# Attention tail of a hyperbolic transformer block: o is scaled ahead of its transpose, TensorE adds the output bias, and the gate product and |a|^2 read the projection from PSUM

## The chip, the cores and the metric

The kernel runs on one core of one Trainium2 chip. A core has five engines that work side by side, each through its own queue in order: TensorE (PE in the profile, with its weight loads as PEld), VectorE (DVE), ScalarE (ACT), GpSimd (POOL) and SyncE (SP, which here issues the DMAs). The metric is the device time of one execution in microseconds, taken as the median of three runs.

## The reference, cut to what matters

Two layers are computed for x of 128 sequences by 64 tokens by 256 features (8192 tokens). Layer 0 is a recurrent scan over the 64 tokens and a quantised feed-forward. Layer 1 is an attention block in hyperbolic space, followed by a small feed-forward and a quantised linear layer. The change lies in the end of the attention:

```
out_h    = expmap0(softmax(q k / 4) v)             # 16 heads of 16 features
attn_out = plin(_from_heads(out_h), w_o, b_o)      # plin: expmap0(logmap0(x) @ w + b)
attn_t   = g_msa * logmap0(attn_out)
x        = mobius_add(residual, expmap0(attn_t))
```

With o the 256 features that leave the softmax for one token, and full a factor for that token that follows from |o|^2, the projection is a = full * (o @ w_o) + b_o. For expmap0 and logmap0 the kernel needs, for every token, |a|^2, the product g_msa * a, and |g_msa * a|^2. They are row sums, one number for each token.

## The kernel before, in words

The tokens are cut into 64 tiles of 128 tokens, and the tiles into 16 groups of 4 (GT = 4), each group into 2 pairs of tiles. A first stage runs the scan, a second the feed-forward of layer 0, and the last, `fused`, does the rest and is the longest.

`fused` is a software pipeline over the groups. Its loop counter k runs from -5 to 18, and in each pass it writes, in this order: `tail(k)` (the residual sums and the scale factors behind attention of group k and behind the small feed-forward of group k - 3), `norms(k)` (layer norm and modulation), `fp6` (the last linear layer of group k - 3), `mlp(k)`, `attention(k + 5)` and `front(k + 6)` (the way in from layer 0). So attention is written five groups ahead of the `tail` that reads it. Written order is not the order of execution: the compiler's scheduler sorts all instructions of an engine by an estimate of their times, with the small coefficient chains (`radial`, `ln_coeffs`, `tail_coeffs`) given priority, and each engine then runs its list strictly in that order. Semaphores hold an instruction until what it reads is written and what it overwrites is free.

PSUM has eight banks, and the table CFG gives them out by name: qk 2, sc 2, ao 1, dn 1, ml 1, fp 1. The one bank called ao serves all of the second half of attention. A group passes through it in this order: for each of its two pairs, the products of the softmax numerators with v, twice (L983, copied out by ACT at L986); then, for each pair, four transposes of o (L92, copied out by ACT at L1005 as oT) and eight projection products with w_o (L1010), which VectorE reads at L1014. Only then can the next group's L983 write the bank.

Between the last L986 of a group and L1014 lies `full`: VectorE divides by the softmax denominator (L988, L989), ScalarE and VectorE sum the squares of o (`square_sum`, L609 and L611), and `radial` on POOL turns the sums into the factor (L653, L640, L655, tiles fullq and fullr).

Behind L1014, `tail_sums` does three things to each tile: a square sum of a on ScalarE (L609), the product with the gate g_msa on POOL (L737, in place), and a square sum of the result on ScalarE. The gate rows `ada` come by DMA (`load_ada`, kind 2 of block 0, two buffers `ada02`). `mlp` calls the same `tail_sums` for its own gate, also on POOL. Later `x_dot` on VectorE (L743) reads the product.

`rows3` is a bf16 tile in whose rows, in groups of three, biases lie as sums of three bf16 parts; a matmul with a matrix of ones from `ones3` as weights adds such a bias in PSUM (L912, L1036, L1092). The output bias b_o is not among them; it lies in `bo`, copied to all partitions, and L1014 adds it.

Of the kernel before, what the change touches and what calls it, by code (L numbers as in the profile page):

```python
# [11 lines left out]
F32 = mybir.dt.float32  # L12
F32R = mybir.dt.float32r
BF16 = mybir.dt.bfloat16
# [3 lines left out]
ALU = mybir.AluOpType  # L18
# [4 lines left out]
P = 128  # L23
B, T, D = 128, 64, 256
# [18 lines left out]
NG = NT // GN  # L43
AR = 8
TS = 4
CFG = {'rnd': 'S', 'ef': 8, 'fill': {'x1a': 'V', 'mod0': 'V'}, 'hold': [3, 0], 'mk': 2, 'raw': 1, 'mv': 6, 'xs': 3, 'la': 3, 'sb': 7, 'qks': 'GGGG', 'deq': 'VV', 'first': 1000, 'hb': 2, 'q_h': 'P', 'q_x1': 'P', 'q_xr': 'P', 'q_ot': 'P', 'q_out': 'P', 'q_ada': 'P', 'room': [[0.3, 0.3, 0.55], [0.5, 0.4, 0.2]], 'qv': 64, 'p1': 'GVGVGVGV', 'x1': 3, 'u1': 16, 'u2': 6, 'qkv': 2, 'sq': 1, 'uT1': 2, 'uT2': 2, 'qM': 2, 'kT': 2, 'e': 4, 'oT': 1, 'yT': 1, 'hq': 2, 'hl': 2, 'xr': 1, 'ot': 2, 'ada00': 2, 'ada02': 2, 'ada10': 2, 'ada12': 4, 'dn': 1, 'qk': 2, 'sc': 2, 'ao': 1, 'ml': 1, 'fp': 1, 'mod0': 'GGGV', 'mod1': 'VVVV', 'sqm0': 'SSSS', 'sqm1': 'SSSS', 'su0': 'VVVV', 'su1': 'VGVG', 'q8': 'GGGGGG', 'hqc': 'SSSVVV', 'qm': 'SSSS', 'x1a': 'GV', 'gate0': 'GGGG', 'gate1': 'GGGG', 'yb': 'GG', 'va': 'GGGG', 'sqt': 'SSSS', 'sqg': 'SSSS', 'sqo': 'SSVS', 'f2e': 'SSSS', 'early': 0, 'q8f': 'VVVVVV', 'hqf': 'SSSVVV', 'fl': 1, 'un': 2, 'jsu': 1, 'LA': 5, 'LM': 3, 'tl': 6, 'ord': 1, 'xt': 3, 'q_xt': 'P'}
GT = 4
NGR = NTILE // GT

LA, LM = CFG["LA"], CFG["LM"]  # L50

# [19 lines left out]
def tile_kernel(ctx, tc, a, out):  # L71
    nc = tc.nc
    V, S, G_, PE = nc.vector, nc.scalar, nc.gpsimd, nc.tensor
    dma = nc.sync.dma_start
# [4 lines left out]
    const = ctx.enter_context(tc.tile_pool(name="const", bufs=1))  # L79
# [14 lines left out]
    ones = const.tile([P, P], F32, name="ones")  # L94
    V.memset(ones, 1.0)

    ones3 = const.tile([P, 3, P], BF16, name="ones3")
    V.memset(ones3, 0.0)
    for n in range(3):
        V.memset(ones3[32 * n : 32 * n + 3, n, :], 1.0)  # L100

    mhead = const.tile([P, 4], F32, name="mhead")
# [2 lines left out]
    wt = ctx.enter_context(tc.tile_pool(name="wt", bufs=1))  # L105
# [4 lines left out]
    wo = wt.tile([P, 2, D], F32, name="wo")  # L110
    wfT = wt.tile([P, 2, D], F32, name="wfT")
    wdT = wt.tile([P, 6, D], BF16, name="wdT")
    bo = wt.tile([P, D], F32, name="bo")
    bf2 = wt.tile([P, D], F32, name="bf2")
    bb2 = wt.tile([P, 1], F32, name="bb2")

    rows3 = wt.tile([P, 2 * D], BF16, name="rows3")
    V.memset(rows3, 0.0)
    sdh = wt.tile([P, D], F32, name="sdh")
    cu = wt.tile([P, 1], F32, name="cu")  # L120
# [21 lines left out]
    with ExitStack() as l0:  # L142
# [15 lines left out]
        with ExitStack() as sc_:  # L158
# [3 lines left out]
            setup = sc_.enter_context(tc.tile_pool(name="setup", bufs=1))  # L162
# [84 lines left out]
            def pieces():  # L247
# [7 lines left out]
                for w, sc, dst in ((a["w_gate"], s_g, wgT), (a["w_up"], s_u, wuT)):  # L255
# [8 lines left out]
                    for j in range(6):  # L264
# [3 lines left out]
                        k = P if j < 5 else 64  # L268
# [7 lines left out]
                for j in range(6):  # L276
                    pt = bank()
                    k = P if j < 5 else 64
# [15 lines left out]
                yield 0, 0.3, 0.5  # L294


                dma(out=bo, in_=a["b_o"].partition_broadcast(P))
                dma(out=bf2, in_=a["b_f2"].partition_broadcast(P))
                dma(out=wo, in_=a["w_o"].rearrange("(c p) k -> p c k", p=P))
                r4 = setup.tile([4, D], F32, name="r4")  # L300
# [94 lines left out]
            for i in range(4):  # L395
                va = ep.tile([P, H, 2, HV], F32, name=f"va{i}", tag=f"va{i}", bufs=1)
# [85 lines left out]
        for b0 in range(0, B, NBB):  # L482
            for c in range(2):

                q8 = xp.tile([P, NBB, T], I8, name="q8", tag="q8")
                src = hsT[:, c, :, b0 : b0 + NBB].rearrange("p t b -> p b t")
# [4 lines left out]
                q8f = q8.rearrange("p b t -> p (b t)")  # L491
# [28 lines left out]
        for tb in range(NG):  # L520
            sl = slice(tb * GN, (tb + 1) * GN)
            for j in range(5):
                pg = ps_a.tile([P, GN], F32, name="pgate", tag="pgate")
                pu = ps_a.tile([P, GN], F32, name="pup", tag="pup")
                for ps, w in ((pg, wgT), (pu, wuT)):
                    for c in range(2):
                        PE.matmul(ps, lhsT=w[:, c, j * P : (j + 1) * P], rhs=xqT[:, c, sl],  # L527
                                  start=(c == 0), stop=(c == 1))
                h_chunk(pg, pu, j, tb, h_d[tb, j])
            if tb % 2:  # L530
# [20 lines left out]
def fused(ctx, tc, a, out_tok, x_tok, L):  # L551
    nc = tc.nc
    V, S, G_, PE = nc.vector, nc.scalar, nc.gpsimd, nc.tensor
# [4 lines left out]
    bo, bf2, bb2, rows3, sdh, cu = (L[k] for k in ("bo", "bf2", "bb2", "rows3", "sdh", "cu"))  # L558
# [46 lines left out]
    def square_sum(e, tag, src, acc):  # L605

        junk = pl.tile([P, D], BF16, name="junk", tag=f"junk{tag}{e}", bufs=1)
        if e == "S":
            S.activation(junk, src, AF.Square, accum_out=acc)  # L609
        else:  # L610
            V.scalar_tensor_tensor(junk, src, 1.0, src, ALU.mult, ALU.mult, accum_out=acc)  # L611

    def scale(e, dst, src, by):

        if e == "S":
            S.activation(dst, src, AF.Copy, scale=by)  # L616
# [113 lines left out]
        for g in range(GT):  # L730
            scale(pick(f"su{which}", g), u[g], u[g], su[:, g : g + 1])

    def tail_sums(av, gb, sums, g, which, tag):

        aa2, ga2, _ = sums
        square_sum(pick("sqt", g), f"t{tag}", av, aa2[:, g : g + 1])
        ENG[pick(f"gate{which}", g)].tensor_tensor(av, av, gb, ALU.mult)  # L737
        square_sum(pick("sqg", g), f"t{tag}", av, ga2[:, g : g + 1])

    def x_dot(xs, av, sums, g, tag):  # L740
# [147 lines left out]
    def attention(i, u, sums):  # L888

        i0 = at[0] = i * GT  # L890
        oall = u
# [106 lines left out]
        for h2 in pairs:  # L998
            pt = bank("ao")
            for i in range(2):  # L1000
                for c in range(2):
                    o = (2 * i + c) * P
                    turn(pt[:, o : o + P], oall[2 * h2 + i][:, c * P : (c + 1) * P])
            oT = big("oT", [P, 4, P])
            S.copy(oT.rearrange("p c t -> p (c t)"), pt)  # L1005
            pm = bank("ao")
            for i in range(2):
                g = 2 * h2 + i
                for c in range(2):
                    PE.matmul(pm[:, i * D : (i + 1) * D], lhsT=oT[:, 2 * i + c, :], rhs=wo[:, c, :],  # L1010
                              start=(c == 0), stop=(c == 1))
            for i in range(2):
                g = 2 * h2 + i
                V.scalar_tensor_tensor(av[g], pm[:, i * D : (i + 1) * D], full[:, g : g + 1], bo,  # L1014
                                       ALU.mult, ALU.add)
                gb = load_ada(0, 2, 1, i0 + g)
                tail_sums(av[g], gb[:, 0, :], sums, g, 0, "a")
        return av

    def mlp(i, u, x2, sums):  # L1020

        i0 = at[0] = i * GT
        fn2 = mk("fn2", GT)
        for h2 in pairs:
            uT = big("uT2", [P, 2, 2, 2 * P], F32R)
            pt = bank("ml")
            for c in range(2):
                for i in range(2):
                    o = (2 * c + i) * P
                    turn(pt[:, o : o + P], u[2 * h2 + i][:, c * P : (c + 1) * P])  # L1030
            S.copy(uT[:, 0], two(pt))
            V.tensor_tensor(uT[:, 1], two(pt), uT[:, 0].bitcast(F32), ALU.subtract)
            for i in range(2):
                g = 2 * h2 + i
                pm = bank("ml")
                PE.matmul(pm, lhsT=ones3[:, 2, :], rhs=rows3, start=True, stop=False)  # L1036
                for k in range(2):
                    cs = slice(k * P, 2 * D)
                    for q, (w, z) in enumerate(PASSES):
                        PE.matmul(pm[:, cs], lhsT=uT[:, z, k, i * P : (i + 1) * P], rhs=wm[:, w, k, cs],  # L1040
                                  start=False, stop=(k == 1 and q == 2))
                junk3 = pl.tile([P, D], BF16, name="junk3", tag="junkz", bufs=1)
                V.tensor_tensor_reduce(out=junk3, in0=pm[:, :D], in1=u[g], scale=1.0, scalar=0.0,
                                       op0=ALU.mult, op1=ALU.add, accum_out=fn2[:, g : g + 1])
                if pick("f2e", g) == "S":
                    S.copy(u[g], pm[:, D:])
                else:
                    V.tensor_copy(u[g], pm[:, D:])
        cf = radial(fn2, "cf", plus=bb2)
        av = u  # L1050
        for g in range(GT):
# [3 lines left out]
            tail_sums(av[g], gb[:, 0, :], sums, g, 1, "m")  # L1055
            x_dot(x2[g], av[g], sums, g, "m")
        return av

# [169 lines left out]
```

## Time and profile before

| what | value |
|---|---|
| median of 3 runs | 1380.88 us (1379.86 to 1386.22) |
| the profiled execution's own time | 1374.36 us |
| its span (first to last instruction) | 1372.6 us |
| busy in the span: DVE, PE, POOL, ACT | 1145.4, 1096.8, 844.6, 827.0 us |
| granted TensorE clock, mean | 0.871 |
| gate products L737 on POOL (attention and mlp) | 128 of 827 ns in the mean |
| projection read L1014 on DVE | 64 of 473 ns in the mean |
| square sums L609 on ACT | 432 of 428 ns, each with a read of the accumulator of 203 ns |

A busy share says how much of the span an engine worked; a wait is the idle time in front of one instruction, put down to the instruction that ended it. In a group's line the columns are: line, engine, operation, names written and read, shapes and count, then busy time, mean ns of one, and idle time before it with what ended it.

### The profile page before, as it was taken

What the parts mean: (1) busy time and instruction counts of PE and PEld (TensorE: products, weight loads), DVE (VectorE), ACT (ScalarE), POOL (GpSimd) and SP (SyncE); (2) the same over time, 40 slices, a digit from 0 to 9 for tenths busy, and PEclk for the clock granted to TensorE, in tenths of its full rate; (3) what the DMA queues carried; (4) which work ended last, traced back from release to release, by engine and by line L of the source; (5) the groups of instructions that cost most, each with busy time, mean ns of one, the idle gap of its engine ahead of it and who ended that gap; (6) DMA issues with size and microseconds to landing.
All of it is one profiled execution on the core that took longest, in us unless ns stands there. A gap on an engine that the chain in (4) does not pass through costs nothing.

```text
span 1372.6 us, 23851 instructions
## 1 busy us (share of the span) xinstructions
PE 1096.8 (80%) x7380; PEld 744.0 (54%) x7380; DVE 1145.4 (83%) x3544; ACT 827.0 (60%) x2428; POOL 844.6 (62%) x1043
## 2 busy tenths in 40 slices
PE   7999957984589789878879798888887888964654
PEld 4656542332366566655657576666655656643442
DVE  5666669997778787888998999999899989899573
ACT  2545438982377568666768666776675777752331
POOL 3111207865688766687868878686686785765441
PEclk9999989995599789889999798997998989986765
DMA  7112245669733441233344334322414231323211
GB/s 236 54 54 85 70 196 195 257 265 283 225 96 120 124 145 49 90 116 117 98 130 125 116 113 146 108 92 90 126 63 124 70 104 51 97 74 96 72 47 46
DMA packets 119306, 163.66 MB, mean 119 GB/s; under 512 B 10885, under 2 KB 72074, under 8 KB 119178
## 3 DMA queue, kind: packets, MB, share of 16 engines
q1 hardware_dynamic: 119178, 162.13, 37.0%
q8 instruction: 58, 0.95, 0.3%
q14 instruction: 70, 0.57, 0.1%
HBM read 115.94 MB, written 46.14 MB: 118 GB/s over the span
## 4 chain that ended last, share of the span: by engine, by line
DVE 44%; PE 21%; POOL 14%; DMA 8%; issue 6%; ACT 6%; SPq 1%; POOLq 0%; DVEq 0%; ACTq 0%
DMA ada<-ada_d 5%; PE pg L434 4%; DVE u L797 4%; PE pg L415 3%; DVE u L724 2%; DVE u L725 2%; DVE junk L743 2%; DVE nh L920 2%; DVE u L618 2%; DVE bn L703 2%; DVE u L1052 2%; POOL r L640 2%; PE pgate L527 1%; PE qk L915 1%; POOL u L737 1%
## 5 line engine op out<-in xcount | busy, mean ns | idle before, releaser
L609 ACT ACTIVATE junk<-u 128x256 bf16<-128x256 f32 x432 | 183.8, 428 | 162.1 <-DVE u L725 49.4
L915 PE MATMUL qk<-wqkv,uT 128*128 128x512 f32 (+1 forms) x768 | 194.8, 391 | 12.3 <-DVE uT L906 6.4
L737 POOL TENSOR_TENSOR u<-u,ada 128x256 f32<-128x256 f32 x128 | 105.7, 827 | 80.9 <-ACT junk L609 73.4
L915 PEld LDWEIGHTS qk<-wqkv,uT 128*128 128x128 f32 x768 | 132.9, 209 | 40.2 <-DVE uT L906 12.1
L966 PE MATMUL sc<-qM,kT 64*64 64x256 f32 x1024 | 128.1, 419 | 20.9 <-ACT kT L956 11.6
L1040 PE MATMUL ml<-wm,uT 128*128 128x512 f32 (+1 forms) x384 | 120.9, 454 | 0.0
L983 PE MATMUL ao<-va,e 128*64 128x34 f32 x2048 | 90.1, 241 | 32.9 <-DVE u L1014 17.8
L983 PEld LDWEIGHTS ao<-va,e 128*64 128x64 f32 x2048 | 79.5, 155 | 59.6 <-DVE u L1014 19.4
L1040 PEld LDWEIGHTS ml<-wm,uT 128*128 128x128 f32 x384 | 83.7, 221 | 47.3 <-issue 25.3
L616 ACT ACTIVATE qM<-sc,mhead 128x256 f32<-128x256 f32 x256 | 102.0, 495 | 11.5 <-PE sc L92 11.3
L880 PE MATMUL dn<-wdT,hq 128*128 128x256 bf16 (+1 forms) x384 | 66.3, 314 | 45.9 <-DVE x L882 20.4
L513 POOL TENSOR_TENSOR hv<-uv,sil 128x512 f32<-128x512 f32 x44 | 57.6, 1312 | 66.2 <-DVE am L516 48.5
L945 POOL TENSOR_TENSOR va<-qkv,comb 64x256 f32<-64x256 f32 x128 | 88.3, 690 | 9.9 <-PE ao L983 4.2
L966 PEld LDWEIGHTS sc<-qM,kT 64*64 64x64 f32 x1024 | 56.5, 143 | 63.1 <-ACT kT L956 17.7
L609 ACT ACTIVATION_READ_ACCUMULATOR junk<-u 128x1 f32 x432 | 87.9, 203 | 0.0
L974 ACT ACTIVATE e<-sc 128x512 f32<-128x512 f32 x128 | 74.7, 606 | 19.4 <-PE ao L983 9.7
L434 PE MATMUL pg<-hsT,WT 128*128 128x128 f32 x504 | 75.3, 289 | 9.4 <-ACT hsT L446 9.0
L434 PEld LDWEIGHTS pg<-hsT,WT 128*128 128x128 f32 x504 | 64.7, 191 | 31.4 <-ACT hsT L446 28.6
L1094 PE MATMUL fp<-wfT,yT 128*128 128x256 f32 x256 | 78.7, 439 | 0.0
L941 POOL TENSOR_TENSOR qkv<-qkv,comb 128x512 f32<-128x512 f32 x64 | 70.2, 1110 | 12.3 <-DVE comb L932 3.0
L620 POOL TENSOR_SCALAR hb<-hl,cu 128x1280 int8<-128x1280 f32 x64 | 64.2, 1008 | 21.4 <-DMA hl<-h_d 14.0
L880 PEld LDWEIGHTS <-hq 128*128 128x128 bf16 (+1 forms) x384 | 37.2, 108 | 73.1 <-issue 37.5
(286 smaller groups left out, 3192.6 us busy)
## 6 DMA issues: line engine op xcount, KB each, us to landing
ada<-ada_d SPq DMA_DIRECT2D x128, 256.0 KB, 3.5
h_d<-hv SPq DMA_DIRECT2D x80, 256.0 KB, 2.1
hl<-h_d SPq DMA_DIRECT2D x32, 640.0 KB, 4.3
ada<-ada_d SPq DMA_DIRECT2D x128, 128.0 KB, 2.4
xt<-in_xT_dram SPq DMA_DIRECT2D x16, 512.0 KB, 4.5
xr<-in_x_dram SPq DMA_DIRECT2D x32, 256.0 KB, 4.3
x_d<-x SPq DMA_DIRECT2D x32, 256.0 KB, 3.1
xt<-x_d SPq DMA_DIRECT2D x32, 256.0 KB, 2.8
```

The costliest lines, as they stand in the source:

```text
L434: lp = PE.matmul(pg[c][:, st], lhsT=WT[:, k, c * P : (c + 1) * P], rhs=hp[:, k, :], start=False, stop=False, skip_group_check=True)
L609: S.activation(junk, src, AF.Square, accum_out=acc)
L616: S.activation(dst, src, AF.Copy, scale=by)
L737: ENG[pick(f"gate{which}", g)].tensor_tensor(av, av, gb, ALU.mult)
L880: PE.matmul(py[:, i * D : (i + 1) * D], lhsT=hq[r, j, i * P : (i + 1) * P], rhs=wdT[r, j, :], start=(i == 0 and j == 0), stop=(j == 5), sk ...
L915: PE.matmul(pm[:, :n_], lhsT=uT[:, z, k, cs], rhs=wqkv[:, w, k, lo:hi], start=False, stop=(k == 1 and q == 2))
L945: ENG[pick("va", g)].tensor_tensor(va[r, :, s, 0:HD], qkv[r, xy, 512:768].rearrange("p (h d) -> p h d", d=HD), bc_in(comb[r, xy * 48 + 32 ...
L966: PE.matmul(sc[rr][s * T : (s + 1) * T, c * 256 : (c + 1) * 256].rearrange("p (v t) -> p v t", v=4), lhsT=kTs[xy][r, c, s * T : (s + 1) * ...
L974: S.activation(e.rearrange("p c v t -> p (c v t)"), sc[rr], AF.Exp, scale=1.0 / math.sqrt(HD))
L983: PE.matmul(pv[xy * T : (xy + 1) * T, hh], lhsT=E[2 * xy + hh // 4][:, c, hh % 4, :], rhs=vas[(2 * h2 + xy) % 4][:, c * 8 + hh], start=Tru ...
L1040: PE.matmul(pm[:, cs], lhsT=uT[:, z, k, i * P : (i + 1) * P], rhs=wm[:, w, k, cs], start=False, stop=(k == 1 and q == 2))
L1094: PE.matmul(o, lhsT=yT[:, 2 * i + c, :], rhs=wfT[:, c, :], start=False, stop=(c == 1))
```

## The change

1. In `attention`, ScalarE multiplies each tile of o by `full` in place, ahead of the transposes (64 new activations of 128x256). VectorE's L1014, which multiplied by `full` and added `bo`, goes.
2. Each projection starts with a matmul of ones with the rows of b_o (64 new bf16 matmuls of 128x256); `ones3` gets a fourth matrix for it.
3. `tail_sums` gets a source of its own: for attention the first square sum and the gate product read the projection in PSUM, and the product writes `av`.
4. The gate product of attention moves from POOL to VectorE (`gate0` from 'GGGG' to 'VVVV'). The one of `mlp` stays on POOL.
5. In the setup, b_o is loaded to one row, split in three by POOL, and brought into `rows3` by three small DMAs; the copy to all partitions goes.

```
-CFG = {... 'gate0': 'GGGG', ...}
+CFG = {... 'gate0': 'VVVV', ...}
...
-    ones3 = const.tile([P, 3, P], BF16, name="ones3")
+    ones3 = const.tile([P, 4, P], BF16, name="ones3")
...
-                dma(out=bo, in_=a["b_o"].partition_broadcast(P))
+                bo = setup.tile([1, D], F32, name="bo")
+                dma(out=bo, in_=a["b_o"].partition_broadcast(1))
+                for i, part in enumerate(split3(bo, 1, G_)):
+                    dma(out=rows3[96 + i : 97 + i, 0:D], in_=part)
...
-    def tail_sums(av, gb, sums, g, which, tag):
+    def tail_sums(av, src, gb, sums, g, which, tag):
         aa2, ga2, _ = sums
-        square_sum(pick("sqt", g), f"t{tag}", av, aa2[:, g : g + 1])
-        ENG[pick(f"gate{which}", g)].tensor_tensor(av, av, gb, ALU.mult)
+        square_sum(pick("sqt", g), f"t{tag}", src, aa2[:, g : g + 1])
+        ENG[pick(f"gate{which}", g)].tensor_tensor(av, src, gb, ALU.mult)
         square_sum(pick("sqg", g), f"t{tag}", av, ga2[:, g : g + 1])
...
         for h2 in pairs:
             pt = bank("ao")
             for i in range(2):
+                g = 2 * h2 + i
+                scale("S", oall[g], oall[g], full[:, g : g + 1])
                 for c in range(2):
                     o = (2 * i + c) * P
                     turn(pt[:, o : o + P], oall[2 * h2 + i][:, c * P : (c + 1) * P])
...
             pm = bank("ao")
             for i in range(2):
-                g = 2 * h2 + i
+                PE.matmul(pm[:, i * D : (i + 1) * D], lhsT=ones3[:, 3, :], rhs=rows3[:, 0:D], start=True, stop=False)
                 for c in range(2):
                     PE.matmul(pm[:, i * D : (i + 1) * D], lhsT=oT[:, 2 * i + c, :], rhs=wo[:, c, :],
-                              start=(c == 0), stop=(c == 1))
+                              start=False, stop=(c == 1))
             for i in range(2):
                 g = 2 * h2 + i
-                V.scalar_tensor_tensor(av[g], pm[:, i * D : (i + 1) * D], full[:, g : g + 1], bo,
-                                       ALU.mult, ALU.add)
                 gb = load_ada(0, 2, 1, i0 + g)
-                tail_sums(av[g], gb[:, 0, :], sums, g, 0, "a")
+                tail_sums(av[g], pm[:, i * D : (i + 1) * D], gb[:, 0, :], sums, g, 0, "a")
```

More of the change, by code (lines that the diff above doesn't have):

```diff
@@ L45 @@
 TS = 4
-CFG = {'rnd': 'S', 'ef': 8, 'fill': {'x1a': 'V', 'mod0': 'V'}, 'hold': [3, 0], 'mk': 2, 'raw': 1, 'mv': 6, 'xs': 3, 'la': 3, 'sb': 7, 'qks': 'GGGG', 'deq': 'VV', 'first': 1000, 'hb': 2, 'q_h': 'P', 'q_x1': 'P', 'q_xr': 'P', 'q_ot': 'P', 'q_out': 'P', 'q_ada': 'P', 'room': [[0.3, 0.3, 0.55], [0.5, 0.4, 0.2]], 'qv': 64, 'p1': 'GVGVGVGV', 'x1': 3, 'u1': 16, 'u2': 6, 'qkv': 2, 'sq': 1, 'uT1': 2, 'uT2': 2, 'qM': 2, 'kT': 2, 'e': 4, 'oT': 1, 'yT': 1, 'hq': 2, 'hl': 2, 'xr': 1, 'ot': 2, 'ada00': 2, 'ada02': 2, 'ada10': 2, 'ada12': 4, 'dn': 1, 'qk': 2, 'sc': 2, 'ao': 1, 'ml': 1, 'fp': 1, 'mod0': 'GGGV', 'mod1': 'VVVV', 'sqm0': 'SSSS', 'sqm1': 'SSSS', 'su0': 'VVVV', 'su1': 'VGVG', 'q8': 'GGGGGG', 'hqc': 'SSSVVV', 'qm': 'SSSS', 'x1a': 'GV', 'gate0': 'GGGG', 'gate1': 'GGGG', 'yb': 'GG', 'va': 'GGGG', 'sqt': 'SSSS', 'sqg': 'SSSS', 'sqo': 'SSVS', 'f2e': 'SSSS', 'early': 0, 'q8f': 'VVVVVV', 'hqf': 'SSSVVV', 'fl': 1, 'un': 2, 'jsu': 1, 'LA': 5, 'LM': 3, 'tl': 6, 'ord': 1, 'xt': 3, 'q_xt': 'P'}
+CFG = {'rnd': 'S', 'ef': 8, 'fill': {'x1a': 'V', 'mod0': 'V'}, 'hold': [3, 0], 'mk': 2, 'raw': 1, 'mv': 6, 'xs': 3, 'la': 3, 'sb': 7, 'qks': 'GGGG', 'deq': 'VV', 'first': 1000, 'hb': 2, 'q_h': 'P', 'q_x1': 'P', 'q_xr': 'P', 'q_ot': 'P', 'q_out': 'P', 'q_ada': 'P', 'room': [[0.3, 0.3, 0.55], [0.5, 0.4, 0.2]], 'qv': 64, 'p1': 'GVGVGVGV', 'x1': 3, 'u1': 16, 'u2': 6, 'qkv': 2, 'sq': 1, 'uT1': 2, 'uT2': 2, 'qM': 2, 'kT': 2, 'e': 4, 'oT': 1, 'yT': 1, 'hq': 2, 'hl': 2, 'xr': 1, 'ot': 2, 'ada00': 2, 'ada02': 2, 'ada10': 2, 'ada12': 4, 'dn': 1, 'qk': 2, 'sc': 2, 'ao': 1, 'ml': 1, 'fp': 1, 'mod0': 'GGGV', 'mod1': 'VVVV', 'sqm0': 'SSSS', 'sqm1': 'SSSS', 'su0': 'VVVV', 'su1': 'VGVG', 'q8': 'GGGGGG', 'hqc': 'SSSVVV', 'qm': 'SSSS', 'x1a': 'GV', 'gate0': 'VVVV', 'gate1': 'GGGG', 'yb': 'GG', 'va': 'GGGG', 'sqt': 'SSSS', 'sqg': 'SSSS', 'sqo': 'SSVS', 'f2e': 'SSSS', 'early': 0, 'q8f': 'VVVVVV', 'hqf': 'SSSVVV', 'fl': 1, 'un': 2, 'jsu': 1, 'LA': 5, 'LM': 3, 'tl': 6, 'ord': 1, 'xt': 3, 'q_xt': 'P'}
 GT = 4
@@ L95, in tile_kernel @@
     V.memset(ones, 1.0)
-    ones3 = const.tile([P, 3, P], BF16, name="ones3")
+    ones3 = const.tile([P, 4, P], BF16, name="ones3")
     V.memset(ones3, 0.0)
-    for n in range(3):
+    for n in range(4):
         V.memset(ones3[32 * n : 32 * n + 3, n, :], 1.0)
@@ L112, in tile_kernel @@
     wdT = wt.tile([P, 6, D], BF16, name="wdT")
-    bo = wt.tile([P, D], F32, name="bo")
     bf2 = wt.tile([P, D], F32, name="bf2")
@@ L557, in fused @@
     wqkv, wm, wo, wfT, wdT = (L[k] for k in ("wqkv", "wm", "wo", "wfT", "wdT"))
-    bo, bf2, bb2, rows3, sdh, cu = (L[k] for k in ("bo", "bf2", "bb2", "rows3", "sdh", "cu"))
+    bf2, bb2, rows3, sdh, cu = (L[k] for k in ("bf2", "bb2", "rows3", "sdh", "cu"))
     ones, ones3, mhead, turn = (L[k] for k in ("ones", "ones3", "mhead", "turn"))
@@ L1054, in mlp @@
             gb = load_ada(1, 2, 1, i0 + g)
-            tail_sums(av[g], gb[:, 0, :], sums, g, 1, "m")
+            tail_sums(av[g], av[g], gb[:, 0, :], sums, g, 1, "m")
             x_dot(x2[g], av[g], sums, g, "m")
```

## The prediction, made before the changed kernel was built

> **What bounds the kernel now.** I read the engine table and the busy tenths of the page first. The busiest engine overall is VectorE, and POOL, which the change relieves, is far from full.
>
> ```profile
> PE 1096.8 (80%) x7380; PEld 744.0 (54%) x7380; DVE 1145.4 (83%) x3544; ACT 827.0 (60%) x2428; POOL 844.6 (62%) x1043
> ...
> DVE  5666669997778787888998999999899989899573
> ...
> POOL 3111207865688766687868878686686785765441
> ```
>
> An average over stages hides the limits, so the table by stretch of the trace comes second (columns: stretch, its length, then PE, PEld, DVE, ACT and POOL busy, clock, DMA). The attention tail runs from 452.6 (first L1014) to 1227.5 (last).
>
> ```profile
> 400.00:650.00 250.00, 213.06 (x1723) 149.78 (x1723) 208.14 (x626) 172.11 (x504) 189.80 (x232) 0.90 0.34 107
> 650.00:1200.00 550.00, 473.07 (x3758) 347.49 (x3760) 514.43 (x1659) 384.13 (x1205) 406.63 (x503) 0.89 0.33 103
> 1200.00:1372.60 172.60, 92.11 (x397) 68.14 (x389) 123.77 (x506) 58.77 (x193) 78.34 (x90) 0.71 0.21 68
> ```
>
> From 650 to 1200 VectorE works 514.43 of 550 us (94%): there it is the limit. From 400 to 650 it works 83% and PE 85%, nothing else more: there a chain sets the pace. Which one shows in the answer for the tile ao, the single PSUM bank of attention's second half, and in the timeline of the third group (columns: start, length, engine, line).
>
> ```profile
>   DVE u L1014: 42.4, 18
> ...
>   PEld ao L983: 27.8, 15
>   PE ao L983: 24.1, 12
> ```
>
> ```profile
> 530.30 0.25 POOL L655 TENSOR_SCALAR fullr<-fullr 128x4 f32<-128x4 f32 x1
> ...
> 531.44 1.89 PE L1010 MATMUL ao<-wo,oT 128*128 128x256 f32 x8
> ...
> 533.44 0.88 DVE L1014 SCALAR_TENSOR_TENSOR u<-ao,fullr,bo 128x256 f32<-128x256 f32 x2
> ...
> 537.74 0.60 PE L92 MATMUL ao<-ident,u 128*128 128x128 f32 x4
> ...
> 545.27 0.87 DVE L1014 SCALAR_TENSOR_TENSOR u<-ao,fullr,bo 128x256 f32<-128x256 f32 x2
> ...
> 546.19 1.13 PE L983 MATMUL ao<-va,e 128*64 128x34 f32 x32 [1.45 <-DVE u L1014]
> ```
>
> The bank is handed on 0.1 us after the last L1014 here, and within 1.3 us in 11 of 15 groups; the next group's softmax numerators (L974) had ended by 530.1, long before. So the bank is hardly ever free, and one group follows another through it. In the first groups the reader follows at once: the last L1014 of groups 0 to 6 ends at 461.3, 506.5, 546.1, 601.5, 652.0, 707.1 and 761.2, and the first rsqrt of `tail` (L640, tile r) starts 10, 19, 6, 19, 16, 27 and 18 us later. For groups 7 to 13 it is 43, 44, 40, 40, 20, 33 and 37 us, for 14 and 15 it is 17 and 9. So the bank's chain sets the pace at both ends, VectorE in the middle.
>
> **What the change saves.** Three terms, all in VectorE's favour.
>
> The read itself: L1014 takes 473 ns in the mean. A two-tensor product of 128x256 with one operand in PSUM isn't in the trace; L444 (128x128, SBUF) has a median of 290 ns, L1032 (128x512, PSUM) one of 679, so by length 290 + 389 x 128/384 = 420 ns. 64 x 53 ns = 3.4 us; bounds 0 (it costs what L1014 does) and 64 x 183 = 11.7 (it costs what L444 does). I take 3.4.
>
> POOL's products: 64 x 827 ns = 53 us leave POOL. Nothing waits for all of it, but VectorE's instructions on SBUF get slower beside POOL, and those that read PSUM do not:
>
> ```profile
> L725 DVE SCALAR_TENSOR_TENSOR u<-u,lnaln,ada x86: 435/479/1553, 337.2 to 1282.2; 128x256 f32<-128x256 f32 x86
> ...
> L1014 DVE SCALAR_TENSOR_TENSOR u<-ao,fullr,bo x64: 424/472/485, 452.6 to 1227.5; 128x256 f32<-128x256 f32 x64
> ```
>
> (min/median/max; L725's mean is 630.) I laid every VectorE instruction from 400 to 1200 beside POOL's starts and ends and took what it has over the median of its kind where POOL is idle: 141 us in all, 30 of them under L737, which has two callers of equal count. Half is 15 us. Bounds: 0, if other POOL work slides into the freed time, and 30. I take 15. [...]
>
> POOL's queue: VectorE waited 16.5 us for the rsqrt r (L758), 5.4 for sur, 13.5 for L737 itself (L743). A shorter queue takes some of that; between 0 and their 35 us I take 5, as most of r's wait is its own 2.9 us.
>
> Together 23 us, worth their price where VectorE is the limit; in the chain-paced 250 + 172 us they mostly become idle time. I count 20.
>
> **What the change adds to the bank's chain.** Before, pair 0's transposes, copy and projection ran beside `full`, and only L1014 waited for it. In the 16 groups the later of `full` and the projection's end comes 0.6 us after `full` in the mean. Now all of it stands behind `full`: two scalings (rows of this size on ScalarE: L956 412, L609 428 ns) 0.86, transposes 0.66, copy L1005 0.61, two bias matmuls at L1092's 0.31 and projection 1.89 together 2.5, four hand-offs of some 0.1: 4.9 - 0.6 = 4.3 us. Pair 1's scaling lies beside pair 0's matmuls and costs nothing; without that cover it is 0.86. Its bias adds 0.6.
>
> Releasing the bank took two L1014, 0.87 us. Now ScalarE (0.43 + 0.20) and VectorE (0.42) each read both halves. Side by side that is 1.26 us, in turns 2.1. The one place where both engines read one bank today, L1043 and L1046 in ml, goes in turns (ScalarE waits there for L1043 30 times, 37.2 us), though L1046 also overwrites an operand of L1043. I take turns: +1.2 us for each pair, 2.4 a group. [...]
>
> The sum is 4.3 + 0.6 + 2.4 = 7.3 us a group, 117 us for 16 if nothing hides it. Two things hide it. Groups 7 to 13 have 20 to 44 us of slack before `tail`. And L1014 waits in VectorE's list after its operands are ready, 1.7 us (pair 0) and 4.2 us (pair 1) in the mean; a later operand first eats that wait. For the nine tight groups I take 7.3 less half of 5.9, 4.3 us, so 39 us. Some 4 us come back once, at the start, since the product that L743 reads no longer queues for a square and POOL behind L1014. Net 35 us. Bounds: 0 (the list absorbs all) and 117.
>
> New waits: L92 waits for a scaling, and behind it in PE's list stand other groups' L915 and L966; the product waits for ScalarE's square, with VectorE's whole list behind it. Like pairs today (L906 and L1032 after a ScalarE copy) cost VectorE 1.2 + 4.7 us for 64, so 6 at most; L988's 6.6 for 32 would make 13. It lies in the 35.
>
> **Off the path.** ScalarE gets 64 x 0.43 = 27 us (70% to 74% in the middle) and loses its waits for L737 (37.1 us for both callers). PE gets 64 x 0.31 = 20 us, in the 2.5 above for the chain, otherwise below VectorE's load. Gate rows in ada02 are freed by the product itself, earlier than by POOL; the loads behind them on SP's queue, for which L724 and L721 waited 19.3 and 26.7 us, may gain up to 10, which I leave in the range. In the setup SP gets three small DMAs that wait for POOL's splitting of b_o, with the scan's loads of x queued behind; the like rows<-s3p landed in 2.2 us and x is loaded two blocks ahead, so nothing, 5 us if that cover fails.
>
> **Sum.** +35 - 20 = +15 us on the profiled 1374.4, so 1389; the median of the runs lies 6.5 above that execution, so 1396.
>
> **Rivals.** (1) VectorE alone decides, and the lists absorb the longer chain: -20 us, with the queue and ada terms -35, so 1346 to 1361. For it: 94% busy in the middle, and the waits in front of L1014. Where part of the chain's cost stays, it gives up to 1374. Against: the bank is hardly ever free, and the first seven tails follow attention closely. It decides once the added chain costs under 20 us, about 1.3 us a group. (2) The chain sets the pace in every group, as the slack of 40 us is used up after six groups: 117 - 23, so up to 1475. For it: numerators wait 20 us and more for the bank. Against: VectorE's own work per group in the middle leaves the chain slack. (3) Both cancel, or the scheduler's new order undoes either: within 0.5%, about what a measurement of this kernel can tell from no change.
>
> **How the numbers follow.** The forecast, a net loss of 8 to 50 us, has 0.42; rival (2) beyond that 0.13; rival (1), from 1346 to 1374, 0.32; cancelling 0.13. So slower by over 0.5% 0.55, same 0.13, faster 0.32. The range from 1356 to 1445 leaves out the far ends of both rivals, a third of (1) and most of (2), 0.1 each. The forecast's own range is 1389 to 1431.
>
> **What would show it.** Right: VectorE's product at 420 ns, POOL down by 50 us, ScalarE up by 27, PE by 20; the groups' passage from fullr to the bank's release longer by 4 to 8 us; the tails still close behind attention in the first groups, and VectorE's idle time from 400 to 650 above its 42 us. Wrong: that passage unchanged, or tails of the first groups no later than now while VectorE's SBUF rows fall towards their medians; then rival (1) holds. A waiting PE L983 in the middle would mean rival (2).

## The result, and the profile after

The changed kernel takes 1463.57 us (median of 6 runs, 1457.92 to 1472.14) against 1380.74 for the kernel before (6 runs, 1378.60 to 1386.22). The ratio is 1.0601, interval 1.0573 to 1.0630: 83 us slower, where 15 had been predicted. The profiled execution took 1463.65 us with a span of 1461.7, 89.1 more than before's. The lines L... of the changed kernel stand two to four below those of before: the projection on TensorE is now L1014 (before, that was VectorE's read), the bias matmul L1012, the gate product L739, the square sum L611, the scaling L618, `fullr` L657.

The engine table and the busy tenths of the changed kernel's page:

```profile
PE 1141.3 (78%) x7444; PEld 768.1 (53%) x7444; DVE 1134.2 (78%) x3545; ACT 856.9 (59%) x2492; POOL 788.1 (54%) x984
...
DVE  5766779977885778888988988988978868867853
...
POOL 3111119756686557676655856657556554535522
```

VectorE has 11 us less to do and POOL 56, as intended, and the kernel is longer all the same: no engine is above 78%. In the tenths, the row of nines that VectorE had in its middle is gone. The table by stretch of the changed kernel (stretch, length, then PE, PEld, DVE, ACT, POOL busy, clock, DMA; attention's tail now runs to 1348):

```profile
400.00:650.00 250.00, 204.96 (x1570) 142.91 (x1569) 189.90 (x582) 161.49 (x474) 173.89 (x208) 0.84 0.36 109
650.00:1300.00 650.00, 540.24 (x3970) 390.37 (x3971) 544.93 (x1789) 434.35 (x1333) 384.69 (x494) 0.84 0.30 92
1300.00:1461.70 161.70, 80.00 (x416) 57.99 (x415) 101.65 (x420) 49.10 (x160) 57.97 (x61) 0.69 0.17 51
```

From 400 to 650 VectorE idles 60 us instead of 42, and in the middle it works 84% of the time instead of 94%: it waits there too now. The answer for the tile ao of the changed kernel says on what. Its first list is what the bank's own users waited for, its second who waited for them:

```profile
its engine sat idle before it (us, times) until:
  DVE u L739: 56.7, 26
...
  PE ao L1014: 23.6, 19
  ACT junk L611: 21.0, 23
...
who waited for it (us, times):
  ACT junk L611: 55.6, 52
...
  PE ao L985: 20.3, 14
  DVE u L739: 19.3, 20
```

The bank's next writer waits for VectorE's product (56.7 us where L1014 made it wait 42.4; weight loads and matmuls are counted apart in both). The product waits for ScalarE's square, 19.3 us, 20 times. ScalarE's 55.6 us are two things, as the rows of the square sums by shape show (line, shapes and count, then busy time and mean ns, then idle time before it with what ended it):

```profile
L611 ACT ACTIVATE junk<-u 128x256 bf16<-128x256 f32 x368 | 155.0, 422 | 159.3 <-DVE u L727 50.6 <-DVE u L739 32.0 <-DVE u L991 31.3
...
L611 ACT ACTIVATE junk<-ao 128x256 bf16<-128x256 f32 x64 | 24.4, 381 | 24.3 <-PE ao L1014 23.6
```

The squares that read the bank wait for the projection, 23.6 us. The 32.0 us for the product stand in front of squares of u in SBUF, among them the one that reads the product's own result. So ScalarE is hardly ever idle for its turn at the bank: while VectorE's product is not yet done, ScalarE works on other entries of its list. The timeline of the third group shows the whole way (start, length, engine, line, x count):

```profile
552.76 0.26 POOL L657 TENSOR_SCALAR fullr<-fullr 128x4 f32<-128x4 f32 x1
...
553.83 1.71 ACT L618 ACTIVATE u<-u,fullr 128x256 f32<-128x256 f32 x4
...
556.88 0.38 PE L92 MATMUL ao<-ident,u 128*128 128x128 f32 x2
...
557.53 1.59 ACT L618 ACTIVATE qM<-sc,mhead 128x256 f32<-128x256 f32 x4
...
560.24 0.67 ACT L1009 COPY oT<-ao 128x512 f32<-128x512 f32 x1
...
564.96 1.03 PE L1014 MATMUL ao<-wo,oT 128*128 128x256 f32 x4
...
566.02 0.38 ACT L611 ACTIVATE junk<-ao 128x256 bf16<-128x256 f32 x1
...
567.68 0.41 DVE L739 TENSOR_TENSOR u<-ao,ada 128x256 f32<-128x256 f32 x1
...
569.73 0.38 ACT L611 ACTIVATE junk<-ao 128x256 bf16<-128x256 f32 x1
...
574.91 0.95 DVE L745 CUSTOM_DVE_ANT_0 junk<-u,u 128x256 bf16<-128x256 f32 x1
575.79 0.41 DVE L739 TENSOR_TENSOR u<-ao,ada 128x256 f32<-128x256 f32 x1
```

Before, `full` ended at 530.55 here and pair 0 had left the bank at 534.32, 3.8 us later. Now it leaves at 576.20, 23.2 us after `full`. None of the eight steps is long. The copy oT stands in ScalarE's list behind another group's scalings (qM). The square of the second half ended at 570.1, but its product starts at 575.79, behind L726, L727, L922, L908, L745 and others that stand ahead of it in VectorE's list and fill that engine without a gap.

I measured this for all 16 groups in the traces, from `full` to the release of pair 0, from there to the release of pair 1, and from that to the first rsqrt of the group's `tail` (the lag). All are means in us; the last two columns are the end of group 15's last read of the bank and what follows it to the end of the span:

| kernel | full to pair 0 released | pair 0 to pair 1 released | lag (range) | last release | drain |
|---|---|---|---|---|---|
| before | 3.1 | 12.9 | 24.9 (5.7 to 43.7) | 1228.0 | 144.6 |
| after | 18.1 | 11.1 | 1.8 (0.8 to 3.4) | 1348.3 | 113.5 |

A group's whole passage through the bank takes 59.6 us in the mean instead of 52.1. Sixteen times that difference (7.44 before rounding) is 119 us; the first group also starts 1.3 us later, and so the last release is 120.3 us later. Behind that release there is 31.1 us less left to do, and 120.3 - 31.1 = 89.2 is the whole loss of the profiled execution. In every one of the 16 groups `tail` now starts within 3.4 us of the release: the bank's chain sets the pace from the first group to the last.

### The profile page after: what moved, and what is told of

Its sections match the earlier page's. It is cut to its first block, busy times and chain, and to the rows that moved or that the text cites. A ratio compares the mean times of both kernels' runs of the same rounds, so it can differ in the third digit from the quotient of the medians.

```text
span 1461.7 us, 23957 instructions
## 1 busy us (share of the span) xinstructions
PE 1141.3 (78%) x7444; PEld 768.1 (53%) x7444; DVE 1134.2 (78%) x3545; ACT 856.9 (59%) x2492; POOL 788.1 (54%) x984
## 4 chain that ended last, share of the span: by engine, by line
DVE 28%; PE 15%; POOL 9%; ACT 6%; DMA 5%; issue 4%; SPq 0%; POOLq 0%; DVEq 0%; ACTq 0%
DMA ada<-ada_d 5%; DVE u L799 4%; PE ml L1042 3%; POOL r L642 2%; PE sc L968 2%; PE qk L917 2%; ACT junk L611 2%; PE ao L985 1%; DVE u L726 1%; PE fp L1096 1%; DVE u L1054 1%; DVE bn L705 1%; DVE junk L745 1%; DVE u L727 1%; PE ao L1014 1%
## 5 line engine op out<-in xcount | busy, mean ns | idle before, releaser
L611 ACT ACTIVATE junk<-u 128x256 bf16<-128x256 f32 x368 | 155.0, 422 | 159.3 <-DVE u L727 50.6
L917 PE MATMUL qk<-wqkv,uT 128*128 128x512 f32 (+1 forms) x768 | 191.8, 392 | 26.9 <-DVE uT L908 18.6
L968 PE MATMUL sc<-qM,kT 64*64 64x256 f32 x1024 | 139.7, 453 | 5.8 <-ACT kT L958 3.8
L985 PE MATMUL ao<-va,e 128*64 128x34 f32 x2048 | 103.4, 258 | 34.3 <-DVE u L739 16.9
L985 PEld LDWEIGHTS ao<-va,e 128*64 128x64 f32 x2048 | 91.8, 175 | 67.6 <-issue 28.2
L882 PE MATMUL dn<-wdT,hq 128*128 128x256 bf16 (+1 forms) x384 | 69.5, 333 | 55.4 <-DVE x L884 30.6
L618 ACT ACTIVATE qM<-sc,mhead 128x256 f32<-128x256 f32 x256 | 101.9, 500 | 6.1 <-PE sc L92 5.9
L968 PEld LDWEIGHTS sc<-qM,kT 64*64 64x64 f32 x1024 | 61.1, 153 | 50.9 <-issue 17.1
L436 PEld LDWEIGHTS pg<-hsT,WT 128*128 128x128 f32 x504 | 65.2, 193 | 32.5 <-ACT hsT L448 30.0
L739 POOL TENSOR_TENSOR u<-u,ada 128x256 f32<-128x256 f32 x64 | 50.6, 791 | 48.4 <-ACT junk L611 44.8
L417 PE MATMUL pg<-xt,WT 128*128 128x512 f32 x128 | 70.5, 638 | 7.4 <-DMA xt<-in_xT_dram 7.4
```

The source lines that it names most:

```text
L417: PE.matmul(pgs[n][c], lhsT=WT[:, 2 + k, sl], rhs=xts[n][:, k, :], start=(n == 0 and k == 0), stop=(k == 1))
L882: PE.matmul(py[:, i * D : (i + 1) * D], lhsT=hq[r, j, i * P : (i + 1) * P], rhs=wdT[r, j, :], start=(i == 0 and j == 0), stop=(j == 5), sk ...
L917: PE.matmul(pm[:, :n_], lhsT=uT[:, z, k, cs], rhs=wqkv[:, w, k, lo:hi], start=False, stop=(k == 1 and q == 2))
L968: PE.matmul(sc[rr][s * T : (s + 1) * T, c * 256 : (c + 1) * 256].rearrange("p (v t) -> p v t", v=4), lhsT=kTs[xy][r, c, s * T : (s + 1) * ...
L985: PE.matmul(pv[xy * T : (xy + 1) * T, hh], lhsT=E[2 * xy + hh // 4][:, c, hh % 4, :], rhs=vas[(2 * h2 + xy) % 4][:, c * 8 + hh], start=Tru ...
```

## The experiments

Every kernel was run beside the kernel before on the same chip; the median of before lay between 1381.0 and 1381.7. Differences from the changed kernel are differences of medians. The scheduler orders each variant anew, so a difference holds the new order along with the edit. Figures for the groups are taken as in the table above.

**1. The scaling alone.** The kernel before, with only the scaling put ahead of the transposes (the first two lines below stand in front of them); VectorE still reads the bank alone and adds bo, the gate product stays on POOL.

```
+                g = 2 * h2 + i
+                scale("S", oall[g], oall[g], full[:, g : g + 1])
...
-                V.scalar_tensor_tensor(av[g], pm[:, i * D : (i + 1) * D], full[:, g : g + 1], bo,
-                                       ALU.mult, ALU.add)
+                V.tensor_tensor(av[g], pm[:, i * D : (i + 1) * D], bo, ALU.add)
```

> The kernel before with one part of the change alone: o is scaled by full ahead of its transpose, VectorE adds b_o out of SBUF as it reads the bank, gate product on POOL as before. Theory (the chain of groups through the one ao bank sets the pace in all 16 groups, and what stands behind full is what lengthened it): the way from full to the release for pair 0, 3.1 us before and 18.1 us after, comes to 10 us or more here, and the time to 1420 to 1450 us, more than half of the loss of 83 us. Rival (the work moved to ScalarE and VectorE costs the time, the order does not): ScalarE only gets its 27 us, VectorE gets nothing, so within 1% of 1381 us.

Measured: 1425.03, ratio 1.0318 (1.0287 to 1.0348). From `full` to pair 0's release it is 13.3 us, the last release is at 1319.1 and the lag 10.7. So the scaling alone is worth 44 us, about half of the loss, and ten of the fifteen us added between `full` and the release.

**2. The gate product alone.** The kernel before with that product on VectorE, from SBUF, behind L1014.

```
-'gate0': 'GGGG'
+'gate0': 'VVVV'
```

> The kernel before with the gate product of attention on VectorE instead of POOL and nothing else; it reads and writes SBUF behind L1014. Theory (the bank's chain): the release is as before, so the time stays within 1.5% of 1381 us, and the passage of a group through the bank within 2 us of 52. Rival (VectorE's list is what the change overloads): 64 products of some 0.5 us more on VectorE, 30 us, of which most is seen: 1400 to 1420 us.

Measured: 1382.14, ratio 1.0004 (0.9983 to 1.0026): nothing, and a group's passage stays at 52.0 us. The engine table of this kernel's page is worth a look:

```profile
PE 1107.9 (80%) x7365; PEld 747.4 (54%) x7380; DVE 1140.9 (83%) x3608; ACT 832.3 (60%) x2428; POOL 794.4 (58%) x979
```

VectorE ran 64 more instructions and was busy 4.5 us less than before's 1145.4; without the 64 products its busy time is 1120.6 us, 25 less. What its instructions took over their medians beside POOL, from 400 to 1200, fell from 141 to 122 us as I sorted them into kinds; other sortings give drops from 4 to 24 us, so the 25 us of busy time are the firmer number. So here the products moved off POOL cost VectorE nothing, and they bring nothing as long as the bank's chain is left as it was.

**3. ScalarE copies the projection out.** The changed kernel with one copy of each pair's bank to SBUF; square and product read that.

```
+            S.copy(av.t[h2].rearrange("p g d -> p (g d)"), pm)
             for i in range(2):
...
-                tail_sums(av[g], pm[:, i * D : (i + 1) * D], gb[:, 0, :], sums, g, 0, "a")
+                tail_sums(av[g], av[g], gb[:, 0, :], sums, g, 0, "a")
```

> The changed kernel, but ScalarE copies the projection of a pair out of PSUM in one instruction, and the square and the gate product read the copy in SBUF. Theory (reading the bank in turns is a part of the lengthened chain: pair 0's four reads take 6.1 us and pair 1's 4.3 us with their waits): one copy of 0.6 us and its wait replace them, so 5 to 7 us of each group's 59.5 come back, 1463 falls to 1360 to 1400 us if the chain still sets the pace, even though ScalarE gets 19 us more. Rival (added work counts): ScalarE has more to do than in the changed kernel, and VectorE's product now has two operands in SBUF: 1463 us or more.

Measured: 1402.91, ratio 1.0166 (1.0140 to 1.0192), 61 us below the changed kernel and just outside the range that I had given. `full` to pair 0 released falls from 18.1 to 11.0 us, though ScalarE has 32 more copies of 0.6 us. From the projection's end to the release, pair 0 now takes 1.1 us and pair 1 1.5, where the reads in turns took 6.1 and 4.6. In the changed kernel, reading the bank in turns cost far more than the four reads are long (2.0 us).

**4. A second ao bank for the changed kernel.** It is taken from qk, so that the table still gives out eight.

```
-'qk': 2, ... 'ao': 1
+'qk': 1, ... 'ao': 2
```

> The changed kernel with two PSUM banks for ao and one instead of two for qk. Theory (one bank, held in turn, is what makes the longer way cost time): the next pair or group need not wait for the release, so at least half of the loss comes back: 1380 to 1425 us, and tail no longer follows attention within 2 us. Rival (the added work, or the longer way from full itself, costs the time whatever the bank): no better than 1450 us, and slower still by what the qk bank was worth.

Measured: 1387.15, ratio 1.0034 (1.0006 to 1.0062): 76 of the 83 us are gone, while `full` to pair 0 is still 15.1 us. Nearly the same long way costs almost nothing when the next user has another bank. The lag is 3.1 us, longer than 1.8 but not the lag of the kernel before; that part of what I expected did not show.

**5. The same for the kernel before.**

> The kernel before with two banks for ao and one for qk, nothing of the change. Theory (the ao bank sets the pace of the first groups and of the last, VectorE that of the middle): a second bank shortens the first groups' passage, VectorE then limits from 400 on, so 1340 to 1375 us. Rival (before the change the bank's chain had slack, and only the longer way made it the limit): within 0.5% of 1381 us, or slower by what the qk bank was worth.

Measured: 1380.17, ratio 0.9984 (0.9957 to 1.0010). My theory expected a gain here and fell; the rival was right. In the kernel before, the bank is hardly ever free, yet relieving it brings nothing by itself, at least not at the price of a qk bank. The groups' releases show where the theory failed: the first three come 17, 28 and 28 us earlier than in the kernel before (461.3, 506.5 and 546.1 there), but the lead is gone by the eleventh, and the last comes at 1247.3 instead of 1228.0. So the one bank did hold up the first groups, and what they gained was lost behind them. A resource that is always occupied is not yet the limit.

**6. One reader, with long reads.** The changed kernel, but ScalarE alone reads the bank: two squares from PSUM, then one copy; the product reads the copy. Called with None, `tail_sums` takes no square of its own and the product reads av.

```
             for i in range(2):
+                g = 2 * h2 + i
+                square_sum("S", "ta", pm[:, i * D : (i + 1) * D], sums[0][:, g : g + 1])
+            S.copy(av.t[h2].rearrange("p g d -> p (g d)"), pm)
...
-                tail_sums(av[g], pm[:, i * D : (i + 1) * D], gb[:, 0, :], sums, g, 0, "a")
+                tail_sums(av[g], None, gb[:, 0, :], sums, g, 0, "a")
```

> The changed kernel, but ScalarE alone reads the projection in PSUM: the two squares as in the changed kernel and then one copy for VectorE's products. Its three reads take 0.58 + 0.58 + 0.61 = 1.8 us by their rows, nearly as long as the four in turns (2.0 us). Theory (the hand-offs between two engine lists cost, not the reading): four waits for the other engine's list fall to one, and it comes near copy_out: 1400 to 1425 us. Rival (the bank's time under reading counts): it stays near the changed kernel, 1445 to 1470 us, since ScalarE also gets 19 us more.

Measured: 1397.22, ratio 1.0112 (1.0067 to 1.0157), 66 us below the changed kernel. Here are its reads in the answer for the tile ao (min/median/max in ns):

```profile
L611 ACT ACTIVATE junk<-ao x64: 362/384/504, 461.0 to 1279.8; 128x256 bf16<-128x256 f32 x64
...
L1022 ACT COPY u<-ao x32: 571/578/716, 461.8 to 1280.2; 128x512 f32<-128x512 f32 x32
```

Two squares, their accumulator reads of 0.19 and a copy are 1.7 us for each pair, three times the single copy of experiment 3, and the time is no longer than there. The reads of the changed kernel are about as long, 2.0 us. From the projection's end to the release it is 2.2 us for pair 0 and 2.0 for pair 1, instead of 6.1 and 4.6. What goes is the changing of engines between the reads: that, more than their length, is what the reads cost.

**7. Without the bias matmuls.** The 64 bias matmuls are left out, so b_o is missing from the result.

```
-                PE.matmul(pm[:, i * D : (i + 1) * D], lhsT=ones3[:, 3, :], rhs=rows3[:, 0:D], start=True, stop=False)
...
-                              start=False, stop=(c == 1))
+                              start=(c == 0), stop=(c == 1))
```

> The changed kernel without its 64 bias matmuls; b_o is left out of the result. Theory: the matmuls stand in the bank's chain with 0.31 us each, 1.2 us a group, less what lies beside the copy: 10 to 20 us less than 1463. Rival (PE's lists, not lengths, decide): within 0.5% of 1463 us.

Measured: 1434.41, ratio 1.0376 (1.0333 to 1.0419): 29 us less, more than the 10 to 20 that I had expected. That is 1.8 us a group, where the length of four matmuls is 1.2; the passage of a group shrinks by 1.4 us. The theory's price by lengths is too low here too, and the rival fell.

**8. Copy out and a second bank** (edits 3 and 4 together).

> Both mends at once: one copy out by ScalarE, and two banks for ao (one for qk). Theory (both shorten the same chain, and VectorE's 1134 us of work, 11 us less than before the change, become the limit): 1350 to 1378 us, faster than the kernel before. Rival (the chain full, scaling, transposes, projection keeps setting the pace through tail's wait for attention, whatever the bank): 1380 to 1395 us, no better than the two banks alone.

Measured: 1370.66, ratio 0.9899 (0.9862 to 0.9936): about 1% faster than the kernel before. The stretch from 650 to 1200 of this kernel:

```profile
650.00:1200.00 550.00, 470.13 (x3722) 342.63 (x3721) 501.51 (x1637) 402.87 (x1236) 364.10 (x453) 0.92 0.34 101
```

VectorE is back at 501.51 of 550 us (91%). That does not show it to be the limit: in experiments 2 and 5, which gained nothing, it works 90% of this stretch.

**9. The scaling alone with a second bank** (edits 1 and 4).

> The kernel with the scaling ahead of the transposes alone (1425 us), now with two banks for ao and one for qk. Theory (the longer way from full costs time because one bank holds up all groups behind it): its loss of 44 us shrinks to less than 15 us, 1380 to 1395 us. Rival (the way from full to tail costs by itself): still 1410 us or more.

Measured: 1396.75, ratio 1.0111 (1.0076 to 1.0146). The 44 us of experiment 1 fall to 15, just above what I had expected at most. The way behind `full` is hardly shorter, 12.3 us instead of 13.3; the bank was what made it dear.

**10. Priority for everything behind `full`.** The changed kernel, with the loop over the pairs put ahead of other work by the scheduler.

```
+        with tc.high_priority(offset=CFG["first"]):
             for h2 in pairs:
```

> The changed kernel, unchanged in work, but the scheduler gives all that stands behind full (scaling, transposes, projection, its squares and products) the priority that the small coefficient chains have. Theory (most of the 18.1 us from full to pair 0's release are waits in the engines' lists, only some 7 us are lengths): the way falls to 10 to 13 us and the time to 1390 to 1430 us. Rival (the hand-offs cost on the chip and no order helps): within 1% of 1463 us.

Measured: 1430.77, ratio 1.0373 (1.0337 to 1.0410), 33 us less, but `full` to pair 0 only falls from 18.1 to 16.0 us. Waits in the lists are a part of the cost that the order can move; the larger part stayed, and both the way (10 to 13 us expected) and the time (up to 1430 expected) lie above the theory's ranges. Of the 10.0 us that pair 0 still stands between two steps, the engine whose turn is next is busy with other instructions for 9.2.

**11. One reader with a second bank** (edits 6 and 4).

> ScalarE alone reads the projection, and ao has two banks, qk one. Theory: like copy_out with two banks, VectorE is the limit: 1355 to 1378 us. Rival (ScalarE's list is full now): 1385 us or more.

Measured: 1379.26, ratio 0.9984 (0.9961 to 1.0007), no different from before, and 1 us above my range. With two banks the longer reads of one reader are 9 us dearer than the single copy (1379.26 against 1370.66), where with one bank they were 6 us cheaper (6 against 3). With one bank the two intervals overlap, so only the difference with two banks is clear.

**12. The kernel before with the gate on VectorE and a second bank** (edits 2 and 4).

> The kernel before with the gate product on VectorE and two banks for ao, one for qk, no scaling ahead and no bias on PE. Theory (what makes copy_out with two banks faster than the kernel before is less work for VectorE and POOL in the read and the gate, not the banks, which alone gave nothing): the 64 products on VectorE stay a cost here, 1370 to 1385 us. Rival (freeing POOL of the product is the gain): 1355 to 1368 us.

Measured: 1370.18, ratio 0.9930 (0.9908 to 0.9952), at the lower edge of the theory's range, but not by its mechanism: the theory had the 64 products stay a cost, and the kernel is as fast as experiment 8 with far less changed. Each edit alone brought nothing (1.0004 and 0.9984); together they bring 11 us. Which relief counts beside the second bank, POOL's 50 us of experiment 2 or VectorE's 4.5, no run separates.

## Why the prediction was wrong, point by point

**What bounds the kernel.** Right in naming the bank's chain, wrong in how I drew the border. I read "the bank's chain at both ends, VectorE in the middle" as if VectorE in the middle protected the groups there. Experiments 5, 2 and 12 show limits that lie close together: a second bank alone brings nothing, the gate product off POOL alone nothing, both 0.7%. That the other limit is VectorE is not shown: it works 94% of the middle before, 90% in experiments 2 and 5, and the gate product's move relieves POOL far more than VectorE.

**What it saves.** The sizes were near. The product and the row that stands for what VectorE loses beside POOL, from the source lines of the changed kernel:

```profile
L739 DVE TENSOR_TENSOR u<-ao,ada x64: 384/414/426, 463.3 to 1347.9; 128x256 f32<-128x256 f32 x64
...
L727 DVE SCALAR_TENSOR_TENSOR u<-u,lnaln,ada x86: 451/479/1553, 338.6 to 1398.3; 128x256 f32<-128x256 f32 x86
```

The product takes 415 ns in the mean (420 predicted). L727's mean falls from 630 to 613 ns, its median stays at 479. What VectorE loses beside POOL fell from 141 to 99 us from 400 to 1200; in the changed kernel that stretch also holds fewer groups, so the 25 us of experiment 2 are the cleaner number, against the 15 taken. The three waits for POOL's queue, 35 us before, came to 32.0 (28.8 in experiment 2), where 5 us of gain had been taken. The loads queued behind the gate rows gained nothing: VectorE waited 30.2 us for them at L726, where it had waited 19.3 at the same place (L724) before. POOL lost 56 us (50 predicted), ScalarE gained 30 (27). PE gained 44 us instead of 20: 64 bias matmuls of 297 ns are 19, and the rest is other matmuls that took longer (L985 258 ns in the mean instead of 241, the granted clock 0.837 instead of 0.871). So a part of the loss may be slower matmuls: L985 keeps TensorE busy 103.4 us where it was 90.1. No run holds the clock fixed to tell. None of the saving shows at the end as a term of its own; with VectorE at 84% in the middle, it was no longer the limit there.

**What it adds to the bank's chain.** The sum was 7.3 us a group, 117 us for 16; measured were 7.4 and 120.3. (The terms behind `full` that the prediction lists add to 5.0 us, not 4.9; the 0.1 changes nothing.) The total is right, its parts are not:

| part of a group's passage | predicted | measured |
|---|---|---|
| `full` to pair 0 released | +5.5 (4.3, and 1.2 of reads in turns) | +15.0 |
| pair 0 to pair 1 released | +1.8 (0.6, and 1.2) | -1.8 |
| products with v and the work up to `full` | 0 | -5.1 |
| hand-on to the next group | 0 | -0.6 |

Behind `full`, pair 0 now takes 18.1 us: to the scaling 1.2, to the transposes 2.1, these 0.9, to the copy 1.8, to the projection 3.9, this 2.1, and the four reads with the waits between them 6.1. Counted by the lengths of the instructions and 0.1 us for each of four hand-offs it was 7 (4.9 and 2.1). The other 11 us are waits in the lists of three engines. I added up, over the 16 groups, the time from the end of one step of pair 0 to the start of the next: 12.0 us a group, 4.5 in front of ScalarE, 4.7 in front of TensorE, 2.8 in front of VectorE. For 11.2 of these 12.0 us the engine whose turn was next was busy with other instructions. The sizes of the single instructions were near: the scaling 533 ns in the mean (430 predicted), the copy and the bias matmul as predicted. The reads go strictly in turns, in all 64 cases: sorted by start, the 128 reads of the bank by L611 and L739 alternate, and each starts at least 0.12 us after the end of the one ahead of it. So the turns were as predicted; the length of the four reads, 2.1 us, was my price, and 6.1 and 4.6 us from the projection's end to the release of the two pairs was the measured one (the 4.3 that I wrote for pair 1 in the expectation of experiment 3 counts from the start of its first read). Why the phases ahead of `full` became 5.1 us shorter stays open: with VectorE and POOL relieved in experiment 2 they take 34.8 us, and 35.0 before, so that relief alone does not do it. So the agreement of the two totals owes something to chance.

**"Two things hide it": the step that failed.** It took 117 us down to 35. The first cover was slack: groups 7 to 13 had 20 to 44 us before their `tail`, so I charged only nine groups. But slack is a stock, and delay through a single bank adds up: what group 3 is late, group 4 is late as well. The lag of the changed kernel is 0.8 to 3.4 us everywhere, so the stock was used up, and once only. What came back is the 31.1 us of shorter drain: in it VectorE is busy 65.2 us instead of 96.5, and that difference is all of it. Work of earlier groups that used to be left over behind the last release had now been done before it, and group 15's own lag fell from 9.2 to 0.8 us. The second cover was L1014's wait in VectorE's list, of which I let half absorb the added time. For pair 1 that held: from the projection's end to the release it takes 4.6 us, where it took 5.0 with one reader. For pair 0 it did not: each new hand-off behind `full` brought a list wait of its own, 12.0 us together, where the prediction had put 0.1 for each of four.

**Rival (2)** describes what happened: the chain sets the pace in every group, 117 less a saving, up to 1475 against 1463.57. I gave it 0.13, because VectorE's own work in the middle "leaves the chain slack". VectorE was busy 94% of that stretch, which is some 49 of the 52.1 us of a passage. A passage that grows by 7.3 us is 10 us longer than VectorE's work for a group, so VectorE could not have stayed the limit unless waits inside the passage shrank by as much. This comparison, from numbers that stood in my own text, was not made. Rival (1) fell on the mark that I had given for it: the tails of the first groups are later, not earlier. The added wait of the product on ScalarE was put at 6 us, at most 13, and measures 19.3.

**What the runs show of the cause.** The loss needs both halves: a way behind `full` that is long because it passes through the lists of several engines, and one bank that is held through all of it. Shortening the way by one reader takes back 61 to 66 us (3 and 6), a second bank 76 with the way still 15.1 us long (4). The scaling alone costs 44, the bias 29. These do not add up to 83, as they are terms of one queue. Open remain how much of the 16 us that are left under priority (10) is order and how much the engines' real load, what share the lower clock has, and whether the lost qk bank costs something by itself: no run gave ao a second bank without taking one from qk. Reading the bank from both engines side by side was not tried.

## What to carry to other kernels

Where groups follow one another through a single buffer that is hardly ever free, compare the time for which a group would hold it after a change with the busiest engine's work for a group (here 59.6 against some 49 us): where holding is longer, every group pays what is added, and slack further down is spent once and not for each group. Work moved from before a late operand to behind it should be priced by the number of hand-offs between engines, each with its list, and not only by its instructions' lengths; here that was 18 us for 7. In this kernel one engine as the only reader of the shared PSUM bank, copying out before others use the data, was the cheaper way with one bank and with two.

## What the runs showed of the hardware that was not expected

VectorE became less busy (1145.4 to 1140.9 us) when it was given 64 more products that had been POOL's (experiment 2): the rest of its work took 25 us less, L725 for one 595 ns in the mean instead of 630, with its median as before. ScalarE's scaling of an SBUF tile in place (f32 to f32) took 533 ns in the mean (508 in the median) where the square sum of the same shape, which writes bf16, took 428 in the kernel before (L609) and 422 in the changed one (L611).

The granted TensorE clock was 0.843 in the mean of the changed kernel's executions (0.834 to 0.851), 0.867 to 0.872 for the kernel before in the three sets of runs, and 0.885 in the two fastest kernels (experiments 8 and 12). It does not simply follow the kernel's time: experiments 6 and 9 both take 1397 us, at 0.849 (0.843 to 0.858) and 0.873 (0.867 to 0.877). No run says what sets it.
